# Four graph layers on one core: empty list entries of the GAT layers skipped by their gathers, and their weight factors set to zero in the buffer

## The chip, the cores and the metric

The kernel runs on one core of a Trainium2 chip. The metric is the device time of one execution in microseconds (us); the kernel before took 3435.26 us, the median of three runs (3429.68 to 3435.46).

## What is computed

The input is a batch of 8 graphs' features, x of shape (8, 2048, 128), and one adjacency matrix of 2048 x 2048 that all share, in which an entry is nonzero with probability 1/128. Four layers follow each other. Layers 0 and 1 are graph attention with 8 heads, a feed-forward part and two layer norms. Layers 2 and 3 are the GAT layers, and the change is in them:

```python
h = x @ W
s_i = h @ a_src
s_j = h @ a_dst
e = s_i[:, :, None] + s_j[:, None, :]
e = jnp.where(e >= 0, e, NEG_SLOPE * e)
e = jnp.where(adj[None, :, :] == 0, -jnp.inf, e)
att = jax.nn.softmax(e, axis=-1)
att = jnp.nan_to_num(att, nan=0.0)
out = jnp.einsum('bij,bjd->bid', att, h)
y = out + x
mu = jnp.mean(y, axis=-1, keepdims=True)
var = jnp.mean((y - mu) ** 2, axis=-1, keepdims=True)
return ln_gamma * (y - mu) * jax.lax.rsqrt(var + LN_EPS) + ln_beta
```

A node thus sums the rows h of its neighbours, some 16 on the average, with weights that are a softmax over these neighbours.

## The kernel before, in words

**Lists in place of a matrix.** A first phase (`start`, L862) reads the adjacency matrix, counts each node's neighbours and sorts the 2048 nodes by that count, largest first. The sorted nodes form 16 tiles of 128, one node to a partition. For each tile t, `find_lists` (L349) writes the neighbours of its nodes into `lists`, which has CAPS[t] columns (slots) for that tile: from 30 in tile 0 down to 11 in tile 15, 277 in all. In tile 0 the last two slots are folded: they hold what single nodes have beyond 28. A node with fewer neighbours than slots has empty entries at the end of its list; their index is N = 2048, one past the last node.

**Tables.** For each layer there is a table in the chip's memory with a row per node (`tables`, L306), and the row holds all 8 graphs of the batch. In layers 0 and 1 it has 2048 elements (8,192 bytes). In layers 2 and 3 it has 1040 (4,160 bytes): 8 x 128 of h, and then 16 weight factors, exp(s) and exp(0.2 s) for each graph. The tables of layers 2 and 3 have one row more, number 2048, which `start` fills with zeros (L1031).

**Gathers.** `gather` (L319) is an indirect DMA issued on GpSimd's queue: for each partition it fetches the table row that its entry of one slot names. `bounds_check` is the highest allowed index; an entry above it is not fetched and raises no error. It is N - 1 for layers 0 and 1, so that an empty entry (N) is skipped, and N for layers 2 and 3, so that an empty entry fetches the row of zeros, whose factors of zero give it the weight zero.

**Buffers and chunks.** Slots are worked on in chunks: of up to 2 slots in layers 0 and 1, of up to 4 in layers 2 and 3 (75 chunks a layer). A chunk lies in one of six buffers `kv`, used in turn (`buffer`, L144). `fetch` (L1080) issues the gathers, up to four chunks ahead, as soon as the table rows that a chunk may need are written.

**A GAT chunk** (`gat_chunk`, L728) does this. VectorE multiplies the second factors by the node's own (L745), takes the larger of the two factors as the weight (L746, and once more for the last two graphs, L751), and multiplies h by the weights for graphs 0 to 5 (L757). ScalarE does the same for graphs 6 and 7, one slot and graph at a time (L762). VectorE adds the second half of the slots to the first (L766). TensorE adds the results into an accumulator in PSUM (L772).

**A tile's tail.** After a tile's last chunk come the sums of the weights (L455 to L462), the division (L649) and `gat_tail` (L778): residual and mean on TensorE (L793 to L802), squares on ScalarE (L809), the power -1/2 on GpSimd (L836), the scaling on ScalarE (L817). In layer 2 the rows for layer 3 are made next and written to its table by an indirect DMA on GpSimd's queue (`put_rows`, L494). In layer 3 VectorE multiplies by gamma and adds beta (L850, L852), and an indirect DMA on GpSimd's queue writes the output (L854). There is one buffer `rows` for this, so ScalarE's next squares, which it also takes, wait until the output write before has read it.

**Order.** The order of all instructions on each engine is the order in which the program issues them (`manual_schedule`, L1206; loop in `layers`, L1153). In each step of that loop a chunk's two first parts are issued (with L745 to L751, then L757 and L762), after them the add and the matmuls of the chunk before, and in between one step of every running tail and of `fetch`. GpSimd's queue so holds gathers, table and output writes and the powers of the tails, in order.

Of the kernel before, what the change touches and what calls it, by code (L numbers as in the profile page):

```python
# [8 lines left out]
F32 = mybir.dt.float32  # L9
# [8 lines left out]
P = 128  # L18
B, N, D = 8, 2048, 128
# [9 lines left out]
NB = 8  # L29
CHUNK = 4 * NB * (D + 2)  # L30
KVB = 6
# [51 lines left out]
def sparse_path(ctx: ExitStack, tc: tile.TileContext, ins: dict, out: bass.AP, flag: bass.AP):  # L83
# [10 lines left out]
    nc = tc.nc  # L94
    const = ctx.enter_context(tc.tile_pool(name="const", bufs=1))
    work = ctx.enter_context(tc.tile_pool(name="work", bufs=2))
    small = ctx.enter_context(tc.tile_pool(name="small", bufs=2))
    dram = ctx.enter_context(tc.tile_pool(name="dram", bufs=1, space=bass.MemoryType.DRAM))
# [4 lines left out]
    def misc():  # L103
        return pm.tile([P, 512], F32, tag="m", name="m")
# [9 lines left out]
    nc.vector.tensor_scalar_add(center, ident, -1.0 / P)  # L114
    onesc = const.tile([P, 1], F32, name="onesc")
    nc.vector.memset(onesc, 1.0)
    half = const.tile([P, 8], F32, name="half")
    nc.vector.memset(half, -0.5)

# [21 lines left out]
    bufs = [const.tile([P, CHUNK], F32, name=f"kv{i}") for i in range(KVB)]  # L141
    turn = [-1]

    def buffer():  # L144
        turn[0] += 1
        return bufs[turn[0] % KVB]
# [155 lines left out]
    def width(l):  # L302
        return NB * (2 * D if l < 2 else D + 2)


    tables = [dram.tile([N + (l > 1), width(l)], F32, name=f"table{l}") for l in range(4)]  # L306

    x_rows = ins["x_nodes"]

# [9 lines left out]
    def gather(l, index, dst):  # L319
        nc.gpsimd.indirect_dma_start(  # L320
            out=dst, out_offset=None, in_=tables[l][:, :],
            in_offset=bass.IndirectOffsetOnAxis(ap=index, axis=0),
            bounds_check=N - (l < 2), oob_is_err=False,
        )

    def transpose4(src):
# [115 lines left out]
    def folded_sums(w, box):  # L442

        columns = w.shape[-1]
        ps = misc()[:, :columns]
        for i in range(FOLD):
            nc.tensor.matmul(ps, merge, w[:, i, :], start=i == 0, stop=i == FOLD - 1)
        box["folded"] = small.tile([P, columns], F32, tag="folded", name="folded", bufs=1)
        nc.scalar.copy(box["folded"], ps)
# [275 lines left out]

    def gat_chunk(l, c):  # L728
        box, t, k, ns = c["box"], c["t"], c["k"], c["ns"]
        mine = own[:, t, :]  # L730
        if c["folded"]:
            pf = misc()[:, :NB]
            nc.tensor.matmul(pf, spread, mine, start=True, stop=True)
            mine = small.tile([P, NB], F32, tag="mine", name="mine", bufs=1)
            nc.scalar.copy(mine, pf)
            yield
        if k == 0:
            box["acc"] = pacc.tile([P, NB // 4, 512], F32, tag="acc", name="acc")
            at, n = (0 if t % 2 == 0 else 512 - NB * CAPS[t]), CAPS[t]
            box["w"] = pair[:, at : at + NB * n].rearrange("p (s b) -> p s b", b=NB)  # L740
        acc, w = box["acc"], box["w"]
        hs = c["buf"]
        wc = w[:, k : k + ns, :]
        wa, wb = hs[:, :, NB * D : NB * (D + 1)], hs[:, :, NB * (D + 1) :]
        nc.vector.tensor_mul(wb, wb, mine[:, None, :].to_broadcast([P, ns, NB]))  # L745
        nc.vector.tensor_max(wc, wa, wb)  # L746
        if c["folded"]:
            box["wf"] = small.tile([P, FOLD, NB], F32, tag="wf", name="wf", bufs=1)
            nc.vector.tensor_max(box["wf"], wa, wb)
        ws = small.tile([P, 4, SCALED], F32, tag="ws", name="ws", bufs=3)  # L750
        nc.vector.tensor_max(  # L751
            ws[:, :ns, :], wa[:, :, NB - SCALED :], wb[:, :, NB - SCALED :]
        )
        yield
        hv = hs[:, :, : NB * D].rearrange("p s (b c) -> p s b c", b=NB)
        nv = NB - SCALED
        nc.vector.tensor_mul(  # L757
            hv[:, :, :nv, :], hv[:, :, :nv, :], wc[:, :, :nv, None].to_broadcast([P, ns, nv, D])
        )
        for i in range(ns):  # L760
            for b in range(nv, NB):
                nc.scalar.mul(hv[:, i, b, :], hv[:, i, b, :], ws[:, i, b - nv : b - nv + 1])  # L762
        yield
        left = -(-ns // 2)
        if ns > 1:
            nc.vector.tensor_add(hv[:, : ns - left], hv[:, : ns - left], hv[:, left:ns])  # L766
        yield
        if c["folded"]:
            folded_sums(box["wf"], box)
        for i in range(left):  # L770
            for j in range(NB // 4):
                nc.tensor.matmul(  # L772
                    acc[:, j, :], merge if c["folded"] else ident, hv[:, i, 4 * j : 4 * j + 4, :],
                    start=k + i == 0, stop=c["last"] and i == left - 1,
                )
        yield
# [85 lines left out]
    def start():  # L862
# [165 lines left out]
        )  # L1028
        for i in (3, 4, 5):
            nc.scalar.copy(bufs[i], nil.to_broadcast([P, CHUNK]))  # L1030
        for l in (2, 3):  # L1031
            nc.sync.dma_start(tables[l][N : N + 1, :], bufs[5][:1, : width(l)])


    def verdict():
# [27 lines left out]
    every = []  # L1063
    blocks = [[{} for _ in range(NT)] for _ in range(4)]
    for l in range(4):
        per = 2 if l < 2 else 4
        for t, k, ns, folded in pieces(l, per):
            c = dict(l=l, t=t, k=k, ns=ns, folded=folded, box=blocks[l][t])
            c["last"] = not folded and k + ns == (CAPS[t] if t > 0 else BASE)
            c["run"] = (attention_chunk if l < 2 else gat_chunk)(l, c)  # L1070
            every.append(c)
    now = [0, 0]
# [7 lines left out]
    def fetch():  # L1080

        while now[1] < len(every):
            c = every[now[1]]
            l, t, k, ns = c["l"], c["t"], c["k"], c["ns"]

            if now[1] - now[0] > (4 if now[1] >= KVB and every[now[1] - KVB]["l"] > 1 else 3):
                return
            resorted = l > 0 and t < 2 and not c["folded"]
            need = NT - max([b for end, b in EARLY[t] if k + ns <= end] + [0] if resorted else [0])
            if put[l] < need:  # L1090
                return
            c["buf"] = buffer()[:, : ns * width(l)].rearrange("p (s c) -> p s c", s=ns)
            for i in range(ns):
                at = t * BASE if resorted else first[t]
                index = (sorted_lists if resorted else lists)[:, at + k + i : at + k + i + 1]
                gather(l, index, c["buf"][:, i])
            now[1] += 1
# [6 lines left out]
    def slot():  # L1104
        advance(threads)
        advance(tails)
        fetch()
        beat[0] += 1
        if beat[0] % 3 == 0 and hurry():
            advance(tails)  # L1110
# [42 lines left out]
    def layers():  # L1153
        threads.append(find_lists(0))
        state(0, 0)
        drain()
        fetch()
        begin(every[0])
        drain()
        threads.append(find_lists(1))  # L1160
        for i in range(len(every) + 2):
            now[0] = i
            fetch()
            c2, c1, c, n1, n2 = (chunk(i + j) for j in range(-2, 3))
            if c["k"] == 0:
# [40 lines left out]
    with tc.manual_schedule():  # L1206
        start()
        layers()
# [521 lines left out]
```

## Time and profile before

| | |
|---|---|
| median of three runs | 3435.26 us |
| the profiled execution | 3404.58 us |
| its span, first to last instruction | 3402.8 us |
| VectorE, TensorE, GpSimd, ScalarE busy | 90%, 81%, 65%, 42% of the span |
| mean granted clock of TensorE | 0.918 |
| moved by DMA | 986.52 MB, 290 GB/s |
| read from memory, written | 937.16 MB, 91.55 MB |
| layer 2, from its first product L757 to the first gather of layer 3 that waited for its last writes | about 2,231 to 2,773 us |
| layer 3 | from there to the end |

Profile and trace are of one execution. In them PE is TensorE's matmuls, PEld its weight loads, DVE VectorE, ACT ScalarE, POOL GpSimd; L757 is line 757 of the kernel before. A group of instructions is shown as line, engine, operation, output<-inputs with their shapes, and the count after an x; behind the bar its busy time in us and the mean ns of one, then the idle time of the engine just before these instructions, and what ended most of it. In a timeline the first two columns are start and duration in us. In a list of waits the columns are the total in us, the number of times, and the longest. The buffers `kv0` to `kv5` are all called kv.

### The profile page before, as it was taken

Reading aid. Unit: us, or ns where it says so; the run is one execution under the profiler, and the core shown is the slowest. Engines: PE = TensorE matmul, PEld = TensorE weight load, DVE = VectorE, ACT = ScalarE, POOL = GpSimd, SP = SyncE. Lnnn points to the kernel's source line nnn. Section 1 sums busy time; section 2 is a strip of 40 time slices with the busy share of each in tenths; the row PEclk is TensorE's granted clock in tenths of the full one; section 3 lists DMA queues with packets and bytes.
Section 4 is the critical chain, followed back from the end, with each engine's and each line's share of the span. In section 5 each row is a group of like instructions: output and inputs, shape, how many; then the busy total and the mean of one; then the engine's idle time right before and its main releaser. Section 6 shows DMA issues by size and latency. Waiting matters only on the chain.

```text
span 3402.8 us, 34669 instructions
## 1 busy us (share of the span) xinstructions
PE 2743.1 (81%) x10618; PEld 1582.9 (47%) x10618; DVE 3058.3 (90%) x2695; ACT 1426.6 (42%) x4972; POOL 2207.9 (65%) x1453
## 2 busy tenths in 40 slices
PE   5647888878989997788888989986888976667675
PEld 4523445545555553455545555653445543233332
DVE  7789999999999999999999999976788866889885
ACT  5711333334444442233333444543555654444444
POOL 0065788588657655455676666646787865788773
PEclk9878999999999998899999999998899988888887
DMA  8587787888888777688887888767999986899883
GB/s 336 188 333 266 292 292 282 314 298 288 308 315 299 290 262 295 226 328 295 303 321 295 295 309 299 265 206 250 321 352 346 347 327 223 292 314 330 300 284 112
DMA packets 200625, 986.52 MB, mean 290 GB/s; under 512 B 31918, under 2 KB 33712, under 8 KB 128436
## 3 DMA queue, kind: packets, MB, share of 16 engines
q0 software_dynamic: 175024, 890.45, 72.4%
q1 hardware_dynamic: 20502, 75.52, 5.9%
q10 hardware_dynamic: 4904, 18.24, 1.4%
q8 instruction: 87, 1.43, 0.2%
q14 instruction: 108, 0.88, 0.1%
HBM read 937.16 MB, written 91.55 MB: 302 GB/s over the span
## 4 chain that ended last, share of the span: by engine, by line
DVE 32%; PE 25%; issue 18%; DMA 10%; POOL 5%; ACT 3%; POOLq 0%; DVEq 0%; ACTq 0%
DVE kv L620 11%; DVE kv L606 11%; PE acc L630 8%; PE acc L772 6%; DMA kv<-table,lists 4%; POOL kv L320 3%; DMA kv<-table,sorted_lists 3%; DVE sc L609 2%; PE m L712 2%; DVE kv L766 2%; DMA table<-rows,perm 2%; DVE kv L757 2%; PE m L329 2%; DVE sums L455 1%; DMA out_dram<-rows,perm 1%
## 5 line engine op out<-in xcount | busy, mean ns | idle before, releaser
L320 POOL DMA_INDIRECT kv<-table,lists x955 | 1450.0, 1518 | 357.2 <-issue 206.7
L630 PE MATMUL acc<-kv,ident 128*128 128x512 f32 x2200 | 1107.7, 634 | 222.1 <-DVE kv L620 221.9
L772 PE MATMUL acc<-kv,ident 128*128 128x512 f32 x1184 | 610.1, 667 | 188.6 <-DVE kv L766 155.4
L630 PEld LDWEIGHTS acc<-kv,ident 128*128 128x128 f32 x2200 | 413.7, 202 | 655.1 <-issue 367.5
L606 DVE TENSOR_TENSOR kv<-kv,q 128x2048 f32<-128x2048 f32 (+1 forms) x282 | 629.2, 2231 | 18.7 <-DMA kv<-table,lists 9.7
L609 DVE TENSOR_REDUCE sc<-kv 128x128 f32<-128x2048 f32 (+1 forms) x284 | 634.0, 2232 | 9.2
L620 DVE TENSOR_TENSOR kv<-kv,w 128x2048 f32<-128x2048 f32 (+1 forms) x284 | 631.4, 2223 | 4.9 <-ACT w L615 4.8
L772 PEld LDWEIGHTS acc<-kv,ident 128*128 128x128 f32 x1184 | 243.6, 215 | 504.7 <-issue 285.1
L757 DVE TENSOR_TENSOR kv<-kv,pair 128x3072 f32<-128x3072 f32 (+1 forms) x150 | 466.1, 3108 | 1.0
L476 POOL TENSOR_TENSOR rs<-ss,half 128x4 f32<-128x4 f32 x128 | 221.2, 1728 | 325.4 <-ACT n L471 324.6
L766 DVE TENSOR_TENSOR kv<-kv 128x2048 f32<-128x2048 f32 (+1 forms) x150 | 296.0, 1974 | 129.0 <-ACT kv L762 129.0
L762 ACT ACTIVATE kv<-kv,ws 128x128 f32<-128x128 f32 x1108 | 339.0, 406 | 163.7 <-DVE ws L751 105.5
L471 ACT ACTIVATE n<-m,eps 128x128 f32<-128x128 f32 x512 | 181.0, 366 | 427.1 <-PE m L712 217.4
L615 ACT ACTIVATE w<-sc,lmask 128x64 f32<-128x64 f32 x554 | 165.0, 351 | 455.3 <-DVE sc L609 454.7
L320 POOL DMA_INDIRECT kv<-table,sorted_lists x153 | 204.9, 1339 | 113.0 <-PE acc L630 41.3
L480 ACT ACTIVATE n<-m,rs 128x128 f32<-128x128 f32 x512 | 146.0, 370 | 109.4 <-POOL rs L476 109.0
L494 POOL DMA_INDIRECT table<-rows,perm x57 | 100.2, 1758 | 134.6 <-ACT rows L545 33.5
L329 PE MATMUL m<-ident,n 128*128 128x128 f32 x640 | 106.2, 288 | 73.5 <-ACT n L817 57.2
L712 PE MATMUL m<-w_L_w,hT 128*128 128x128 f32 x1024 | 156.2, 275 | 0.0
L329 PEld LDWEIGHTS m<-ident,n 128*128 128x128 f32 x640 | 82.3, 147 | 140.6 <-ACT n L817 69.0
L712 PEld LDWEIGHTS m<-w_L_w,hT 128*128 128x128 f32 x1024 | 134.9, 192 | 0.0
L691 PE MATMUL m<-n1T,w_L_gnn_W 128*128 128x512 f32 x256 | 131.5, 597 | 0.8 <-ACT n1T L686 0.4
(241 smaller groups left out, 3459.5 us busy)
## 6 DMA issues: line engine op xcount, KB each, us to landing
kept<-xT SPq DMA_DIRECT2D x48, 512.0 KB, 7.4
xT<-kept SPq DMA_DIRECT2D x48, 512.0 KB, 6.8
kv<-in_adj_dram SPq DMA_DIRECT2D x16, 1024.0 KB, 6.7
table<-kv ACTq DMA_DIRECT2D x16, 1024.0 KB, 5.0
kv<-table,lists POOLq DMA_INDIRECT x955, 7.1
kv<-in_x_nodes_dram SPq DMA_DIRECT2D x16, 512.0 KB, 5.8
kv<-table,sorted_lists POOLq DMA_INDIRECT x153, 6.3
found<-cand POOLq DMA_DIRECT2D x16, 64.0 KB, 4.0
```

Of the source, the lines that this page charges most:

```text
L320: nc.gpsimd.indirect_dma_start(out=dst, out_offset=None, in_=tables[l][:, :], in_offset=bass.IndirectOffsetOnAxis(ap=index, axis=0), bound ...
L329: nc.tensor.transpose(pt[:, j * P : (j + 1) * P], src[:, j, :], ident)
L476: nc.gpsimd.tensor_tensor(rs, ss, half[:, :4], op=ALU.pow)
L606: nc.vector.tensor_mul(kk, kk, q[:, None].to_broadcast([P, ns, NB, D]))
L609: nc.vector.tensor_reduce(sc[:, :ns].rearrange("p s (b h) -> p (s b) h", h=NH), kk.rearrange("p s b (h j) -> p (s b) h j", h=NH), axis=AX. ...
L620: nc.vector.tensor_mul(vv, vv, w[:, k : k + ns, :].rearrange("p s (b h) -> p (s b) h", h=NH)[:, :, None, :] .to_broadcast([P, ns * NB, HD, ...
L630: nc.tensor.matmul(acc[:, j, :], merge if c["folded"] else ident, kv[:, i, 4 * j : 4 * j + 4, D:], start=k + i == 0, stop=c["last"] and i ...
L712: nc.tensor.matmul(y[:, j, :], hT[:, f, j, :], wt["2"][:, f, :], start=False, stop=f == 1, skip_group_check=True,)
L757: nc.vector.tensor_mul(hv[:, :, :nv, :], hv[:, :, :nv, :], wc[:, :, :nv, None].to_broadcast([P, ns, nv, D]))
L762: nc.scalar.mul(hv[:, i, b, :], hv[:, i, b, :], ws[:, i, b - nv : b - nv + 1])
L766: nc.vector.tensor_add(hv[:, : ns - left], hv[:, : ns - left], hv[:, left:ns])
L772: nc.tensor.matmul(acc[:, j, :], merge if c["folded"] else ident, hv[:, i, 4 * j : 4 * j + 4, :], start=k + i == 0, stop=c["last"] and i = ...
```

## The change

In layers 2 and 3 an empty entry is no longer fetched. The bounds check of every gather is N - 1, and the row of zeros, with the two small DMAs that wrote it, is gone. In the place of an empty entry the buffer now keeps what it held. So that its weight is zero all the same, the 16 factors of all four slots of a buffer are set to zero after use: `gat_weights` is a view of these 4 x 16 columns, and a copy on ScalarE from a constant zero column, issued after the products L762 of the chunk, clears them for the buffer's next turn. The first six chunks of layer 2 find buffers that layer 1 used; for these a memset on GpSimd, ahead of the chunk's gathers, clears the factors. The h part of an empty entry is whatever was there and is multiplied by zero.

```diff
+    nought = const.tile([P, 1, 1], F32, name="nought")
+    nc.vector.memset(nought, 0.0)
...
-    tables = [dram.tile([N + (l > 1), width(l)], F32, name=f"table{l}") for l in range(4)]
+    tables = [dram.tile([N, width(l)], F32, name=f"table{l}") for l in range(4)]
...
-            bounds_check=N - (l < 2), oob_is_err=False,
+            bounds_check=N - 1, oob_is_err=False,
...
+    def gat_weights(buf):
+
+        return buf[:, : 4 * width(2)].rearrange("p (s c) -> p s c", s=4)[:, :, NB * D :]
+
     def gat_chunk(l, c):
...
         for i in range(ns):
             for b in range(nv, NB):
                 nc.scalar.mul(hv[:, i, b, :], hv[:, i, b, :], ws[:, i, b - nv : b - nv + 1])
+
+        nc.scalar.copy(gat_weights(c["whole"]), nought.to_broadcast([P, 4, 2 * NB]))
         yield
...
-        for l in (2, 3):
-            nc.sync.dma_start(tables[l][N : N + 1, :], bufs[5][:1, : width(l)])
...
-            c["buf"] = buffer()[:, : ns * width(l)].rearrange("p (s c) -> p s c", s=ns)
+            c["whole"] = buffer()
+            c["buf"] = c["whole"][:, : ns * width(l)].rearrange("p (s c) -> p s c", s=ns)
+            if l == 2 and every[now[1] - KVB]["l"] == 1:
+                nc.gpsimd.memset(gat_weights(c["whole"]), 0.0)
```

## The prediction

> **What bounds the kernel now.** I read the page first, then the busy time by window inside the two GAT layers (2,225 us to the end), then the waits of VectorE there, and last the timelines at the places where a wait ends on a DMA. From the page, the whole run and the queue that the change makes lighter:
>
> ```profile
> PE 2743.1 (81%) x10618; PEld 1582.9 (47%) x10618; DVE 3058.3 (90%) x2695; ACT 1426.6 (42%) x4972; POOL 2207.9 (65%) x1453
> q0 software_dynamic: 175024, 890.45, 72.4%
> L757 DVE TENSOR_TENSOR kv<-kv,pair 128x3072 f32<-128x3072 f32 (+1 forms) x150 | 466.1, 3108 | 1.0
> L762 ACT ACTIVATE kv<-kv,ws 128x128 f32<-128x128 f32 x1108 | 339.0, 406 | 163.7 <-DVE ws L751 105.5
> ```
>
> VectorE is the fullest engine. The 150 GAT chunks take 150 L757 products and 1108 ScalarE products L762. Windows of layer 2 (first two) and layer 3 (third); columns are busy us of PE, PEld, DVE, ACT, POOL, then TensorE clock, DMA share, GB/s:
>
> ```profile
> 2500.00:2700.00 200.00, 176.39 (x673) 98.10 (x673) 177.57 (x190) 118.08 (x464) 161.21 (x124) 0.97 0.96 349
> 2700.00:2760.00 60.00, 57.74 (x253) 34.41 (x252) 53.01 (x65) 40.29 (x160) 49.21 (x39) 1.00 0.97 365
> 3050.00:3350.00 300.00, 223.45 (x560) 102.47 (x559) 258.93 (x278) 133.09 (x517) 225.64 (x166) 0.86 0.87 299
> ```
>
> The DMA engines look full (0.96) in layer 2, and that would promise much. But a full resource bounds only if someone waits for it. VectorE's waits from 2,225 us on (total, times, longest):
>
> ```profile
> DVE kv L766 <- ACT kv L762: 129.0, 39, 10.8
> DVE kv L745 <- DMA kv<-table,lists: 40.4, 9, 23.7
> DVE rows L850 <- ACT rows L817: 35.9, 13, 12.2
> DVE o L649 <- PE acc L772: 18.7, 13, 6.2
> DVE kv L745 <- DMA kv<-table,sorted_lists: 17.2, 9, 8.9
> ```
>
> Gathers end only 57.6 us of it, and of that 34.8 are three waits at 2,267, 2,285 and 2,327 us, where layer 2 still waits for its table to be written, and 7.1 is the same at 2,870. About 15.7 us are landings late by 1 to 2.4 us. Most waits are for ScalarE, which stands in order behind two things: the GpSimd power of a tail (161 us of ScalarE's waits), and in layer 3 the landing of the output write (111.5 us). So the GAT layers are held by VectorE, with GpSimd's queue close behind.
>
> **What the Trainium skill says.** DMA: Bandwidth & Descriptors, The descriptor swizzle: a transfer of 128 partitions gives every one of the 16 engines 8 fixed partitions, 0-63 to engines 0-7. No view here shows engines, but it matters: nodes are sorted by degree, so empties sit in high partitions and engines 0-7 are relieved least. ScalarE: Activation LUTs, What ACT_TABLE_LOAD costs: an activation with immediates takes 186 ns + 0.833 ns an element, and back-to-back ones overlap by 93 ns. The trace agrees roughly: the 128x8 copy L547 has a median of 187 ns, the 128x64 Exp with a bias operand 351. GPSIMD Engine Reference, 8. Key points: GpSimd shares its SBUF interfaces with VectorE, with contention under instructions of two SBUF inputs. The trace agrees: of the 134 GAT gathers that took over 1.2 us to issue (median of all 0.997), 104 began while the two-input add L766 ran. Issue time therefore isn't set by the number of rows; gathers of wholly empty and full lists have the same median in layer 3 (0.993 and 1.000).
>
> **Part 1, rows not fetched.** Counted from the inputs, a layer's lists have 277 x 128 = 35,456 entries for 32,733 edges: 2,723 empty (7.7%), 9 slots wholly empty, always a tile's last one. The trace's DMA records have 75,776 packets of 4,160 bytes: 2 x 35,456 gathered and 4,864 written rows, so empties move today. Of 8,192 bytes there are 67,898: 2 x 32,733 gathered and 2,432 written, so layers 0 and 1 do skip theirs by the same bounds check, and the change will work. It removes 5,446 packets, 22.7 MB; at a mean of 0.188 us on 16 engines that is 64 us of DMA time. By the swizzle the least relieved engine loses 101 of 2,216 packets a layer: 2 x 101 x 0.188 = 38 us for both. A wholly empty gather landed 2.1 us after issue in layers 0 and 1 at its quickest, against about 7.0 in layers 2 and 3. Where does this reach the end?
>
> (a) Hand-over of layer 2 to 3. GpSimd's timeline:
>
> ```profile
> 2760.59 0.99 POOL L320 DMA_INDIRECT kv<-table,lists  x1 [0.30 <-issue]
> 2761.88 0.99 POOL L320 DMA_INDIRECT kv<-table,lists  x1 [0.30 <-issue]
> 2763.18 2.48 POOL L494 DMA_INDIRECT table<-rows,perm  x1 [0.31 <-issue]
> 2773.28 1.02 POOL L320 DMA_INDIRECT kv<-table,sorted_lists  x1 [7.62 <-DMA table<-rows,perm]
> ```
>
> The table write lands 9.3 us after issue behind three gathers with 46, 98 and 128 empties; elsewhere 4.3 with quiet queues. On engines 0-7 these drop from 24 packets to about 12: 12 x 0.166 (median packet) = 2.0 us. GpSimd, the power behind it, ScalarE and VectorE (10.8 us idle at 2,785.6) all follow. -2.0 (0 to -2.8).
>
> (b) The end. The same three lists stand ahead of an output write, on which ScalarE and then VectorE wait:
>
> ```profile
> 3341.42 1.01 POOL L854 DMA_INDIRECT out_dram<-rows,perm  x1 [0.30 <-issue]
> 3348.15 0.37 ACT L809 ACTIVATE rows<-m,eps 128x128 f32<-128x128 f32 x1 [12.23 <-DMA out_dram<-rows,perm]
> 3353.39 2.29 DVE L766 TENSOR_TENSOR kv<-kv 128x2048 f32<-128x2048 f32 x1 [4.04 <-ACT kv L762]
> ```
>
> It lands in 6.6 us against 4.4 for the last but one, at 3,379.6: -1.8 (0 to -2.2).
>
> (c) Four late landings at 2,696 to 2,744, 5.8 us together, where tiles 12 to 14 end in wholly empty slots and DMA is at 0.97. TensorE (57.7 of 60 busy) is late next, so I take half: -3.0 (0 to -5.8). (d) The wait of 2.4 at 2,990.5 ends when the wholly empty slot of tile 3 lands; the slot before was issued 1.3 earlier: -1.2 (0 to -2.4). (e) The chunks of tile 0 with 93 to 115 empties a slot, waits 0.97 and 1.16: half, as GpSimd's issue is late next: -1.0. (f) Output writes of layer 3 directly behind a nearly empty gather (at 3,019, 3,085, 3,115); those at 3,189 to 3,310, where VectorE waits longest, have full lists ahead and gain nothing: -2.0 (0 to -4). Sum -11.0.
>
> **Part 2, ScalarE's copy, 128x64, once a chunk.** Not in the trace. Price by the skill 186 + 53 - 93, about 0.15 us in a row; from above 0.35 (the Exp). I take 0.25: 150 x 0.25 = 37.5 us of ScalarE. It follows the products L762, needs nothing that they don't need, and lies beside L757: 8 products take 2.45, the product on VectorE 3.35, so 0.25 fits into 0.9. Behind it on ScalarE stand the tail's squares, copies and the next chunk's products. Without cover, where ScalarE is already late (39 + 13 waits), each costs up to 0.25: 13. Most of these follow an idle stretch of ScalarE in which the copy has long run, so +2.0 (0 to 13). A gather's wait moves from a product to the copy behind it, of a chunk that is over when the buffer comes round: 0.
>
> **Part 3, six memsets on GpSimd** ahead of layer 2's first gathers. Nearest row: memset L870, 128x64, 0.141: 0.85; with the contention above up to 2.3 each: 14. They wait only for VectorE's reads, which the gather behind them waits for as well; queued behind are gathers, table writes and powers. GpSimd is idle for 57 of 100 us there: +0.5 (0 to 14). **The rest**: one memset at the start, two 4 KB writes gone from SP's queue, a table shorter by a row: 0, hidden by the first phase's loads; without that cover under 0.5.
>
> **Sum.** -11.0 + 2.5 = -8.5 against the profiled execution's 3404.58 (span 3402.8 and 1.8 around it): 3396.1. The median of the runs, 3435.26, lies 30.7 higher; I carry the difference over: 3426.8.
>
> **Rivals.** *DMA sets the pace*: the share of 0.96 speaks for it, the few waits on landings against. Whole effect on the least relieved engine 38 us; with two thirds of it, 25: 3410. *Hidden by prefetch*: four chunks are ahead, and each shortened wait is refilled by GpSimd's issue or TensorE; the 129 us for ScalarE speak for it. Gain 1: 3434. *Slower*: the copy stands between the products and the add L766. That decides once it ends after L757, so if it is ordered behind L757 as writing the same buffer, or starts over 0.65 us late: 0.25 and about 0.1 of hand-over in half the chunks, 75 x 0.35 = 26, less 11: 3450. Against it: L762, too, writes between L757's columns, and at 3,111.43 both begin at once.
>
> **Numbers.** Forecast 0.50 (own range 3420 to 3434), DMA pace 0.16, hidden 0.22, slower 0.12. The measurement tells about 0.2% (6.9 us) from no change. Of the forecast 0.6 lies below 3428.4, with DMA's pace: faster 0.46. Its other 0.4 and hidden: same 0.42. Slower 0.12. The range 3410 to 3440 leaves out the slower case and half of DMA's.
>
> **What would show it.** 4,160-byte packets 70,330; q0 at 867.8 MB; the wait at 2,773 down from 7.6 to about 5.6; the four at 2,696 to 2,744 halved; L762's count and L766's 129 us about as before. I am wrong if L766 waits much longer for ScalarE, if the copy takes over 0.4 us, or if the time between layers grows.

## The result, and the profile after

| | before | after |
|---|---|---|
| median, us | 3434.22 | 3427.71 |
| runs, lowest to highest | 19, 3424.04 to 3441.48 | 19, 3417.52 to 3437.23 |
| ratio, 95% interval | | 0.9978, 0.997 to 0.9987 |
| the profiled execution: time, span | 3404.58, 3402.8 | 3428.15, 3426.3 |

The ratio says 7.6 us less (4.5 to 10.3 by its interval); 8.5 were forecast. The two profiled executions differ the other way, and must not be subtracted: judged by TensorE's clock, their chips were not alike. In the series below the kernel before took 3434.87 us on one chip, and 3407.16, 3407.92 and 3405.7 on others. Between the profiled executions it is layer 2 that makes the difference, and there TensorE's granted clock differs. The windows of layer 2, of the kernels before and after, show it (columns as in the prediction: after the lengths PE, PEld, DVE, ACT, POOL, then TensorE clock, DMA share, GB/s):

```profile
2230.30:2788.60 558.30, 453.31 (x1756) 258.42 (x1756) 436.25 (x463) 300.15 (x1163) 406.02 (x318) 0.91 0.87 310
```

```profile
2235.80:2818.50 582.70, 475.82 (x1756) 272.43 (x1756) 436.13 (x462) 311.49 (x1237) 403.67 (x322) 0.88 0.81 278
```

The second is 24.4 us longer with 22.5 us more of PE for the same 1,756 matmuls, and a clock of 0.88 for 0.91. This would hide the change. So the profile after is read against that of a kernel of experiment 3, which has the change's copies but skips nothing and ran at the same clock:

```profile
2232.60:2820.80 588.20, 472.69 (x1756) 271.04 (x1755) 436.26 (x462) 311.29 (x1237) 405.59 (x323) 0.88 0.83 295
```

Against this, layer 2 is 5.5 us shorter in the changed kernel, in one execution of each, at 278 GB/s in place of 295: by these figures some 7% less data and 1% less time.

Lines moved: the products L757 and L762 are now L762 and L767, the add L766 is L773, the squares L809 are L816, and the copy is L769. The page after, on the lines that the prediction began with:

```profile
PE 2765.5 (81%) x10618; PEld 1596.4 (47%) x10618; DVE 3058.6 (89%) x2696; ACT 1448.9 (42%) x5122; POOL 2216.0 (65%) x1459
q0 software_dynamic: 175024, 867.82, 70.6%
L762 DVE TENSOR_TENSOR kv<-kv,pair 128x3072 f32<-128x3072 f32 (+1 forms) x150 | 466.2, 3108 | 1.0
L767 ACT ACTIVATE kv<-kv,ws 128x128 f32<-128x128 f32 x1108 | 341.1, 406 | 170.6 <-DVE ws L756 102.1
```

ScalarE has 150 instructions more (the copies), GpSimd six more (the memsets, 0.14 to 0.17 us each, 0.95 together). The queue q0 moves 867.8 MB, as forecast, and the DMA records hold 70,330 packets of 4,160 bytes, exactly the number forecast. The page's count of packets in q0, 175,024, did not change: in the place of a skipped row stands a packet of 4 bytes. The records hold 36,035 of these, and 30,591 before; that is 5,444 more, for 5,446 empty entries. Their median is 9 ns, that of a row 161 ns. The copy's own line (durations: lowest, median, highest ns):

```profile
L769 ACT COPY kv<-nought x150: 226/240/292, 2253.9 to 3383.6; 128x64 f32<-128x64 f32 x150
```

VectorE's waits from 2,225 us on, after:

```profile
DVE kv L773 <- ACT kv L767: 117.5, 34, 10.2
DVE o L650 <- PE acc L779: 36.6, 14, 6.1
DVE rows L857 <- ACT rows L824: 34.8, 13, 11.2
DVE kv L750 <- DMA kv<-table,lists: 33.3, 9, 21.2
DVE kv L750 <- DMA kv<-table,sorted_lists: 21.9, 6, 8.9
```

The add's wait hardly changed: 117.5 us for ScalarE and 14.0 us more for which the list names no releaser, 131.5 together, against 129.0 before. The wait for TensorE's sums (36.6 us for 18.7) goes with the slower clock: the kernel of experiment 3 has 35.8. The two waits on gathers make 55.2 us together, against 57.6: with 7.7% of the rows gone, VectorE waits for rows nearly as long as before. The gain shows most at two places. The first is the hand-over from layer 2 to 3, where the table write of tile 12 stands behind the last gathers of tile 15. GpSimd's timeline:

```profile
2793.28 0.99 POOL L321 DMA_INDIRECT kv<-table,lists  x1 [0.30 <-PE acc L779]
2794.58 0.99 POOL L321 DMA_INDIRECT kv<-table,lists  x1 [0.30 <-issue]
2795.88 1.00 POOL L495 DMA_INDIRECT table<-rows,perm  x1 [0.30 <-issue]
2801.93 1.03 POOL L321 DMA_INDIRECT kv<-table,sorted_lists  x1 [5.04 <-PE acc L779]
```

From the start of the table write (L495) to the next gather it was 10.10 us; it is 6.05. Part of that is the write's own issue, 1.00 for 2.48, which is no effect of the change: the kernel of experiment 3 issues it in 1.00, too, and still takes 9.70. The releaser named here, PE, had long been done; what ended the wait is the landing of the write, whose last packet ended 4.85 us after its issue. The second place is near the end, at the output write of tile 12, which is the fourth last and the last with gathers ahead of it:

```profile
3368.70 1.01 POOL L861 DMA_INDIRECT out_dram<-rows,perm  x1 [0.30 <-issue]
3372.17 0.37 ACT L816 ACTIVATE rows<-m,eps 128x128 f32<-128x128 f32 x1 [8.84 <-DMA out_dram<-rows,perm]
3377.42 2.29 DVE L773 TENSOR_TENSOR kv<-kv 128x2048 f32<-128x2048 f32 x1 [0.81 <-ACT kv L767]
```

From the issue of the output write to ScalarE's squares it was 6.72 us (3,341.42 to 3,348.15 in the prediction's lines); it is 3.47, and VectorE's wait behind it falls from 4.04 to 0.81.

### The profile page after: what moved, and what is told of

Read it like the earlier page. It is cut to its first block, busy times and chain, and to the rows that moved or that the text cites. A ratio compares the mean times of both kernels' runs of the same rounds, so it can differ in the third digit from the quotient of the medians.

```text
span 3426.3 us, 34787 instructions
## 1 busy us (share of the span) xinstructions
PE 2765.5 (81%) x10618; PEld 1596.4 (47%) x10618; DVE 3058.6 (89%) x2696; ACT 1448.9 (42%) x5122; POOL 2216.0 (65%) x1459
## 3 DMA queue, kind: packets, MB, share of 16 engines
q0 software_dynamic: 175024, 867.82, 70.6%
## 4 chain that ended last, share of the span: by engine, by line
DVE 36%; PE 23%; issue 19%; DMA 8%; POOL 5%; ACT 3%; POOLq 0%; DVEq 0%; ACTq 0%
DVE kv L621 13%; DVE kv L607 12%; PE acc L779 8%; PE acc L631 5%; POOL kv L321 3%; DMA kv<-table,lists 3%; DVE sc L610 2%; DVE kv L773 2%; DMA kv<-table,sorted_lists 2%; DVE kv L762 2%; PE m L713 1%; DVE sums L456 1%; PE m L330 1%; PE m L528 1%; DMA out_dram<-rows,perm 1%
## 5 line engine op out<-in xcount | busy, mean ns | idle before, releaser
L762 DVE TENSOR_TENSOR kv<-kv,pair 128x3072 f32<-128x3072 f32 (+1 forms) x150 | 466.2, 3108 | 1.0
L477 POOL TENSOR_TENSOR rs<-ss,half 128x4 f32<-128x4 f32 x128 | 234.9, 1835 | 315.2 <-ACT n L472 314.3
L773 DVE TENSOR_TENSOR kv<-kv 128x2048 f32<-128x2048 f32 (+1 forms) x150 | 296.2, 1975 | 131.6 <-ACT kv L767 117.5
L767 ACT ACTIVATE kv<-kv,ws 128x128 f32<-128x128 f32 x1108 | 341.1, 406 | 170.6 <-DVE ws L756 102.1
L495 POOL DMA_INDIRECT table<-rows,perm x57 | 94.4, 1656 | 130.5 <-ACT rows L546 32.9
```

What stands on the lines that cost most here:

```text
L477: nc.gpsimd.tensor_tensor(rs, ss, half[:, :4], op=ALU.pow)
L762: nc.vector.tensor_mul(hv[:, :, :nv, :], hv[:, :, :nv, :], wc[:, :, :nv, None].to_broadcast([P, ns, nv, D]))
```

## The experiments

Theory, after the result: the gain comes from writes that stood in the DMA queue behind nearly empty gathers, and most of it from tile 15; the copies cost next to nothing. Rivals: a lighter DMA gains everywhere (rows in proportion); the copy's cost eats a larger gain; or the single row of zeros, fetched by 5,446 entries, was itself slow. In the table every ratio is to the kernel before on the same chip.

| | kernel | before, us | us | ratio, 95% interval |
|---|---|---|---|---|
| 1 | only tile 15's empties skipped | 3434.87 | 3427.86 | 0.9979, 0.9971 to 0.9987 |
| 2 | all but tile 15's skipped | 3434.87 | 3429.73 | 0.999, 0.9982 to 0.9999 |
| 3 | copies, nothing skipped | 3434.87 | 3435.72 | 1.0, 0.9991 to 1.0009 |
| 4 | all skipped, no copies | 3434.87 | 3425.32 | 0.9979, 0.9966 to 0.9992 |
| 5 | nearly no row fetched | 3407.16 | 3375.76 | 0.9901, 0.9885 to 0.9917 |
| 6 | before, with 128 rows of zeros | 3407.16 | 3412.08 | 1.0017, 1.0008 to 1.0026 |
| 7 | after, two halves of the output buffer | 3407.16 | 3367.67 | 0.9882, 0.9864 to 0.9899 |
| 8 | before, two halves | 3407.16 | 3367.68 | 0.9881, 0.9864 to 0.9897 |
| 9 | tile 15 of layer 2 only | 3407.92 | 3405.89 | 0.9993, 0.9984 to 1.0002 |
| 10 | tile 15 of layer 3 only | 3407.92 | 3402.58 | 0.9984, 0.9977 to 0.9992 |
| 11 | after, every copy eight times | 3407.92 | 3393.64 | 0.9966, 0.9953 to 0.9979 |
| 12 | two halves, every copy eight times | 3405.7 | 3369.49 | 0.9894, 0.9877 to 0.991 |

**1. Tile 15 alone.** All of the change is kept, and the row of zeros too; the bounds check skips the empties of the last tile only, 610 of the 5,446 rows.

```diff
-            bounds_check=N - 1, oob_is_err=False,
+            bounds_check=N - skip, oob_is_err=False,
...
-                gather(l, index, c["buf"][:, i])
+                gather(l, index, c["buf"][:, i], l < 2 or t == NT - 1)
```

> The changed kernel, with its copies and memsets, but the row of zeros is kept and only the empties of tile 15 are skipped in layers 2 and 3 (610 of 5,446 rows, 11%). Theory (the gain is at the two ends of a layer, where a write stands behind tile 15's nearly empty gathers): 5 to 7 us below the kernel before, table write at the hand-over followed by the next gather after about 6 us, VectorE's wait at the last output write under 1 us. Rival (DMA engines set the pace, every row saved counts alike): 11% of the gain less the copies, so within 2 us of the kernel before.

Measured: 7.2 us less than before (4.5 to 10.0), as much as the whole change with 11% of its rows. Its timelines, GpSimd and ScalarE:

```profile
2789.14 1.00 POOL L495 DMA_INDIRECT table<-rows,perm  x1 [0.30 <-issue]
2795.39 1.02 POOL L321 DMA_INDIRECT kv<-table,sorted_lists  x1 [5.25 <-DMA table<-rows,perm]
...
3372.31 0.37 ACT L816 ACTIVATE rows<-m,eps 128x128 f32<-128x128 f32 x1 [8.84 <-DMA out_dram<-rows,perm]
```

Both waits are as short as in the full change. It follows that rows do not count in proportion: 11% of them would then have given 0.8 us.

**2. All but tile 15.** The same with `t < NT - 1` in place of `t == NT - 1`: 4,836 rows skipped.

> The changed kernel with the row of zeros kept for tile 15 alone: the other 4,836 empties (89%) are skipped. Theory of the two ends: within 3 us of the kernel before, the table write at the hand-over again followed by 10 us of GpSimd's waiting. Rival of DMA pace: 89% of the gain, 5 to 7 us faster.

Measured: 3.4 us less (0.3 to 6.2), for 89% of the rows, so these rows are worth something, too. The wait at the end stays (6.35 us from the output write to the squares), that at the hand-over is between (8.30). The gains of 1 and 2 add up to 10.6 where both at once gave 7.6; the intervals (about 3 us either way on each) are wide enough for that.

**3. Copies alone.** The same with `l < 2`: the copies and memsets stay, every empty entry fetches its zeros.

> The kernel before with the copies on ScalarE and the memsets on GpSimd added, and nothing skipped. Prediction's step: 2.5 us slower than the kernel before. Rival (the copy stands in VectorE's way): 15 to 25 us slower, VectorE's waits for ScalarE's products up by as much from 129 us.

Measured: no difference (within 3.1 us either way). Its timelines at the two places:

```profile
2795.86 1.00 POOL L495 DMA_INDIRECT table<-rows,perm  x1 [0.30 <-issue]
2805.56 1.02 POOL L321 DMA_INDIRECT kv<-table,sorted_lists  x1 [8.70 <-DMA table<-rows,perm]
...
3378.13 0.37 ACT L816 ACTIVATE rows<-m,eps 128x128 f32<-128x128 f32 x1 [11.88 <-DMA out_dram<-rows,perm]
```

Both waits are long again, so they belong to the rows and not to the copies.

**4. No copies.** The change without its copy on ScalarE.

```diff
-        nc.scalar.copy(gat_weights(c["whole"]), nought.to_broadcast([P, 4, 2 * NB]))
```

> The changed kernel without the 150 copies on ScalarE, so that an empty entry counts with the factors that an earlier chunk left in its slot (the GAT sums are then not the reference's). Prediction's step: about 2 us faster than the changed kernel, so 8 to 10 below the kernel before. Rival that the copies cost nothing: equal to the changed kernel, 6 to 7 below. Rival that they cost much: 15 or more below.

Measured: 0.9979 beside 0.9978 with the copies. 3 and 4 agree from both sides that 150 copies of 0.24 us, 36 us of ScalarE, cost nothing that shows (3 us either way in 3, 5 in 4). So a much larger gain that the copies ate is excluded; one of 2 us isn't.

**5. Nearly no row fetched.** The limit of the rival that DMA sets the pace.

```diff
-            bounds_check=N - 1, oob_is_err=False,
+            bounds_check=N - 1 if l < 2 else 0, oob_is_err=False,
...
```

> The changed kernel with a bounds check of 0 in layers 2 and 3, so that their gathers are issued as before but fetch only node 0's row; the factors are set to 0.5 in place of 0 and the flag for the other path is forced off (the results of layers 2 and 3 are left out of the computation: they are made of what lay in the buffers). It shows all that DMA traffic of gathers can be worth in these layers. Theory that landings matter only where a write stands behind gathers or a first gather is waited for: 20 to 50 us below the changed kernel for 92% of the rows, not more, since VectorE, GpSimd's issue and TensorE stay. Rival of DMA pace (7 us for the 8% of the change, in proportion): 80 us or more.

Measured: 33.7 us less than before, about 26 less than the changed kernel (0.9901 / 0.9978), for the whole of the remaining gathers. Its page and VectorE's waits:

```profile
q0 software_dynamic: 175024, 595.93, 48.7%
```

```profile
DVE kv L773 <- ACT kv L767: 123.6, 41, 10.1
DVE kv L750 <- DMA kv<-table,lists: 24.0, 4, 19.8
DVE kv L750 <- DMA kv<-table,sorted_lists: 8.5, 6, 2.1
```

272 MB fewer than after, and the add still waits 123.6 us for ScalarE. If DMA set the pace, 80 us or more were expected. Since all remaining rows together are worth 26 us, 7.7% spread evenly would be worth some 2 (an estimate in proportion): that the change gained 7.6 is a matter of place. Even of the 26 us the larger part is in layer 3. From the start of its first chunk to that of its last this kernel takes 545.5 us and the changed one 562.2, and ScalarE's wait for the output write is 62.5 us in place of 98.0:

```profile
ACT rows L816 <- DMA out_dram<-rows,perm: 62.5, 8, 10.7
```

**6. A row of zeros for each partition,** on the kernel before. Every empty entry fetches row N + p of 128 rows of zeros in place of the one row N.

```diff
+        each = small.tile([P, 48], F32, tag="each", name="each")
+        nc.vector.tensor_scalar(
+            each[:, :s], top[:, :s], 0.0, node[:, 0:1], op0=ALU.is_equal, op1=ALU.mult
+        )
+        nc.vector.tensor_add(far[:, :s], far[:, :s], each[:, :s])
...
```

> The kernel before, nothing skipped, but 128 rows of zeros in place of one: the empty entry of partition p fetches row 2048 + p, so that no two of a gather read the same row. Tells apart why the writes behind tile 15 landed 3.2 to 4 us earlier where 12 packets of 0.166 us on the fullest engine give 2.0. If it is the number of packets alone: same as the kernel before, 6.5 us from the last output write to ScalarE's squares, 9.7 to 10.1 at the hand-over. If reading one row from many packets at once is slow: each about 1 us shorter, no packets of 0.9 us or more behind tile 15's last gathers, and up to 3 us less in all.

Measured: 5.8 us more. The two new groups of instructions cost 7.0 us of VectorE, which is enough to account for it:

```profile
L394 DVE TENSOR_SCALAR each<-top,node 128x18 f32<-128x18 f32 (+12 forms) x16 | 4.2, 263 | 0.0
L397 DVE TENSOR_TENSOR far<-far,each 128x18 f32<-128x18 f32 (+12 forms) x16 | 2.8, 178 | 0.6
```

And the waits stay. At the hand-over, on GpSimd's timeline:

```profile
2773.92 2.48 POOL L499 DMA_INDIRECT table<-rows,perm  x1 [0.30 <-issue]
2783.20 1.02 POOL L320 DMA_INDIRECT kv<-table,sorted_lists  x1 [6.80 <-DVE ws L756]
```

It is 9.28 us from write to gather, and 5.93 from the output write of tile 12 to the squares. These are the shortest of the kernels that fetch all empties (9.66 to 10.10, and 6.51 to 6.79), so a part of up to 0.8 us may be due to the one row; but the skipped rows took off 3. Single packets of 1.1 to 1.8 us remain, too. That one row is read by all is not the main cause of the waits.

**7 and 8. Two halves of the output buffer,** after and before. ScalarE's waits for an output write come from the one buffer `rows`; here even and odd tiles of layer 3 take halves of another buffer, which is idle then.

```diff
-            n = rows_of(box)[:, : B * D].rearrange("p (b d) -> p b d", d=D)
+            n = rows_of(blocks[3][0])[:, t % 2 * B * D : (t % 2 + 1) * B * D]
+            n = n.rearrange("p (b d) -> p b d", d=D)
```

> The changed kernel with layer 3's output rows in two halves of one buffer by turns, so that ScalarE's squares wait for the output write of two tiles before and not of the last. Theory (VectorE waits in layer 3 mostly because ScalarE stands behind the output write): ScalarE's 98 us of waiting for it gone, 20 to 35 us faster than the changed kernel. Rival (the next wait, GpSimd's power or VectorE itself, is right behind): under 7 us faster.

> The same two halves in the kernel before. Theory: 20 to 35 us faster than the kernel before; the change's gain beside it falls by the 3 us of the end, so that the changed kernel with two halves is some 4 us below this one. Rival that the gain is spread over all tiles: 7 us below as without the halves.

Measured: 40 us less in both, 3367.67 and 3367.68, where 20 to 35 were expected. From ScalarE's waits with the change and halves the output write is gone:

```profile
ACT kv L767 <- DVE ws L756: 105.7, 28, 10.2
ACT n L825 <- POOL rs L844: 97.5, 15, 11.0
ACT rows L825 <- POOL rs L844: 80.1, 13, 12.4
```

From the start of layer 3's first chunk to that of its last it is 528.9 and 529.9 us, and was 568.2. Of the change's gain nothing is seen beside the halves, but with these intervals less than some 8 us can't be told, so that this says little on the hand-over. At the end nothing is left to gain, since no one waits for the write: ScalarE takes the next squares without it (their second half begins 1.42 and 1.53 us after its issue).

**9 and 10. The two places apart.** As 1, in layer 2 only (`t == NT - 1 and l == 2`), and in layer 3 only.

> As the kernel that skips tile 15's empties alone, but in layer 2 only (305 rows): the write to layer 3's table is relieved, the last output writes are not. If the 3.7 us that the hand-over's wait lost reach the end: 3 to 4 us below the kernel before, GpSimd's gap at the hand-over 6.2 us, the last output write to ScalarE's squares still 6.5. Rival (layer 3 takes it back, as its first chunks wait for the next table write anyway): 0 to 1 us below.

> The same for layer 3 only (305 rows). If the 3.2 us at the last output write reach the end: 3 us below the kernel before, gap at the hand-over 10 us, output write to squares 3.5. Rival (TensorE's last sums are late anyway): 0 to 1 us below.

Measured: 2.4 us less (5.5 less to 0.7 more), and 5.4 less (2.7 to 7.8). The traces show each wait shortened in its own kernel and long in the other: 6.73 and 9.69 us at the hand-over, 6.78 and 3.46 at the end. The end is shown to reach the time, and the traces agree: the output write after this one follows 18.06 to 18.08 us later in the four kernels with one output buffer and one copy or none that skip these rows, and 20.5 to 21.4 us later in the five that fetch them. The hand-over is shortened, but whether that reaches the time this pair doesn't settle. The traces say that it reaches VectorE: from the hand-over's write to the start of layer 3's fifth chunk it is 64.3 to 65.1 us in five kernels that skip the rows and 65.7 to 68.0 in six that fetch them. Further on the ranges overlap.

**11. Eight copies.** To see how much cover the copy has.

```diff
-        nc.scalar.copy(gat_weights(c["whole"]), nought.to_broadcast([P, 4, 2 * NB]))
+        for _ in range(8):
+            nc.scalar.copy(gat_weights(c["whole"]), nought.to_broadcast([P, 4, 2 * NB]))
```

> The changed kernel with the copy on ScalarE eight times a chunk in place of once. Seven more of about 0.15 us in a row are 1.05 us, so products and copies take 3.6 us beside VectorE's 3.35. Prediction's step (a copy is free while it fits into the 0.9 us that VectorE's product leaves): little for the first five or six, then late, in all 15 to 45 us above the changed kernel. Rival (ScalarE has room everywhere, since it idles half the time): under 5 us. Rival (every copy is on the path): 158 us.

Measured: 0.9966, not slower at all, so the 15 to 45 us more that were expected are excluded. Beside the changed kernel's 0.9978 it is 4 us less, with 5 us either way by the two intervals, so that a gain is not shown. ScalarE's timeline at two chunks of layer 3:

```profile
3199.64 2.18 ACT L770 COPY kv<-nought 128x64 f32<-128x64 f32 x8
3201.72 2.17 ACT L825 ACTIVATE rows<-m,rs 128x128 f32<-128x128 f32 x8
3203.73 2.47 ACT L767 ACTIVATE kv<-kv,ws 128x128 f32<-128x128 f32 x8
3206.07 2.19 ACT L770 COPY kv<-nought 128x64 f32<-128x64 f32 x8
```

Eight take 2.18 us, 0.27 each. The next products start behind them, and VectorE's add doesn't wait longer for it: 116.9 us in all, with 131.5 in the changed kernel, whose trace is of a slower chip.

```profile
DVE kv L774 <- ACT kv L767: 116.9, 43, 10.1
```

What has become less is ScalarE's wait for the output write. The changed kernel, then this one, whose trace is of the quickest of its eight executions:

```profile
ACT rows L816 <- DMA out_dram<-rows,perm: 98.0, 11, 15.1
```

```profile
ACT rows L817 <- DMA out_dram<-rows,perm: 59.0, 9, 11.4
```

**12. Halves and eight copies.** If there is a gain in 11 and it runs through the output write, it must go when no one waits for that.

> The two halves of the output rows and the eight copies together, on the changed kernel. Eight copies alone came out 0.12% of the whole below the changed kernel where 15 to 45 us above were expected, with ScalarE's waits for the output write down from 98 to 59 us. If that is where the gain came from (a later ScalarE meets the output write when it has landed), it is gone here, since with two halves nothing waits for that write: then 5 to 40 us slower than two halves with one copy (0.988 of the kernel before), by what the copies stand in VectorE's way. Rival (the copies help in another way, by evening out TensorE's or the DMA engines' load): again some 10 us faster than the two halves alone, 0.985 or less.

Measured: 0.9894, beside 0.9882 with halves alone (halves and copies 4 us more, 8 either way). A further gain to 0.985 is excluded; so is the larger part of the 5 to 40 us expected. 1,050 more copies of 0.27 us, 284 us of ScalarE, cost between nothing and some 12 us even with the output write out of the way.

## Why the prediction was right, point by point

The sign, the size (8.5 forecast, 7.6 measured, 3 us either way) and the main mechanism were right: writes with a reader stood behind nearly empty gathers. That the sum came so near is in part luck, for single steps missed on both sides: (b) was too small by 1.2 us, (c) too large by 1.3, and the 2.0 us charged for the copies did not show. The waits below are read at the same instruction in the traces of all kernels with one copy or none, experiment 5 left out, as means: those in which the row's empties are fetched (five to seven), and those that skip them (four or five). For (b) they are those with one output buffer.

| step | forecast | kept | skipped | change |
|---|---|---|---|---|
| (a) table write to next gather | -2.0 | 9.46 | 6.42 | -3.0 |
| (a) VectorE's wait behind it | | 9.85 | 7.36 | -2.5 |
| (b) output write to squares; VectorE's wait | -1.8 | 6.5; 3.8 | 3.5; 0.8 | -3.0; -3.0 |
| (c) late rows of tiles 12 to 14, layer 2 | -3.0 | 6.4 | 4.7 | -1.7 |
| (d) slot of tile 3 and the next chunk | -1.2 | 2.5 | 1.2 | -1.3 |
| (e) four chunks of tile 0, both layers | -1.0 | 36.3 | 35.5 | -0.8 |

**(a) and (b), the writes behind empty lists: right, (a) at about its size, (b) too small.** In (a) the traces mix two lengths of the write's own issue, 1.00 and 2.48 us. Among those with the same length VectorE's wait fell by 1.8 and 2.3 us, which is the forecast, and the gap to the next gather by 2.8 and 3.0. (b) was taken from the last but one output write as the floor, 4.4 us. No gathered row stood ahead of that one, but one of its own packets took 1.13 us; in traces where none is that long it takes 3.5. The floor measured for (b) is 3.46 to 3.47, in four kernels.

The packets' records of (b) show the wait itself. Before the change 209 gathered rows still had to start when the write was issued. The last of them ended 5.01 us after that, and the write's last packet 1.25 us later, at 6.26. In the other four kernels that fetch these rows the last row ended at 4.25 to 5.08, and the write again 1.25 later in each. After the change 9 rows were left, and the last ended at 0.56; the write's packets began at 1.58, after all rows, and ended at 3.01. The count "12 x 0.166 = 2.0", made for (a), fell short here: the last row ended about 4 us earlier, not 2, of which the write could use 3. Why it is twice the count stays open. Single long packets don't explain it: before the change 11 of these rows took over 0.4 us, eight of them 0.9 to 1.3, but in experiment 3 four did, none over 0.85, and its write ended at 6.03. The descriptor swizzle of the Trainium skill's DMA: Bandwidth & Descriptors, by which (a) was counted, is seen here as far as start times can tell, for the records name no engine: the last slot that fetches anything has 30 rows, on the first partitions, and these went as about four packets each on 7 to 8 engines, one after the other, with the other engines idle.

**(c) too large, (d) right.** Of the late rows a quarter went, not half. TensorE or GpSimd's issue is not what holds the rest: in experiment 5, which issues the same gathers but fetches next to nothing, these waits are gone. They are for the rows of full entries, which the change leaves.

**(e) wrong in its place.** The wait of 1.16 us in layer 3 belonged to a chunk whose slots have few empties. What did fall was the wait of the folded chunk ahead of these, 23.66 to 21.18 and 7.12 to 4.12, and the next chunk's rose by nearly as much, 1.04 to 3.04 and 1.11 to 4.57. A wait was moved, not removed. **(f) not resolved:** ScalarE's waits for output writes are 97.0 to 101.1 us with all skipped or all but tile 15 and 104 to 120 otherwise in kernels with one buffer and one copy or none, which allows for a good part of the -2.0 to -4, but those of tile 15 are in it.

**The copy: the price right, the cover wrong.** 0.240 us, 0.25 was taken; ScalarE: Activation LUTs, What ACT_TABLE_LOAD costs gives 186 + 53 = 239 ns without the overlap. In a row there is no overlap to be seen, 0.27 each. The cover was said to be 0.9 us beside VectorE's product, and +2.0 to come from where it lacks. Experiments 3 and 4 put the cost at 0, 3 to 5 either way, and 11 shows that 2.2 us per chunk fit. The reason lies in the order of the program: behind a copy stand the next chunk's products and at times a tail's squares or scalings, and the products must be done by the next chunk's add. So the cover is VectorE's whole period of a chunk, about 6 us at the least (3.35 for the product, 2.28 for the add, 0.54 for the weights), less 2.45 for the products, and not the product alone.

**The rivals.** *DMA sets the pace* falls by 5 (26 us for 92% of the rows left) and by 1 against 2. *Hidden by prefetch* is right for most of the other 89% of the rows, which gave 3.4 us in experiment 2, and wrong for tile 15's, behind whose lists there is no prefetch but a write with a reader. *Slower* falls by 3, 4 and 11: the copy does not come between the products and the add. That the change doesn't do what it says falls by the 70,330 packets. (Before it, the records hold 75,778, two more than the prediction's sum, which left out the two writes of the row of zeros.)

**What stays open:** how much of the hand-over's 2 to 3 us reaches the end (2.4, 3 either way); why the last rows behind tile 15 take twice the count, and why single packets are long; and whether eight copies gain anything, and by what steps they shorten ScalarE's wait for the output write.

## What to carry to other kernels

That a resource is 0.96 busy doesn't say what relieving it is worth: ask who waits for it, and look for the few places where something with a reader waiting stands behind the load. Here 11% of the rows, ahead of two writes, gave 7.2 us, and all of them 7.6. The larger lever was another wait, which the prediction had listed: the one output buffer of layer 3, cut into two halves, takes 1.2% off with or without the change (0.9882 and 0.9881), five times as much. When a wait is shortened, look at the next one on the same engine before it is counted: in tile 0 it took back nearly all.

## What the runs showed that was not expected

Work added to ScalarE did not slow the kernel: eight copies a chunk raise its busy time by two thirds in the middle of layer 3. The window of the kernel with eight copies, then of the changed one:

```profile
3000.00:3100.00 100.00, 70.12 (x179) 31.89 (x178) 90.26 (x88) 75.66 (x304) 82.60 (x62) 0.86 0.89 309
```

```profile
3000.00:3100.00 100.00, 69.98 (x183) 31.85 (x182) 87.44 (x90) 45.94 (x184) 83.18 (x60) 0.87 0.90 309
```

ACT goes from 45.94 to 75.66 us, and the other engines' busy times stay within 3 us. And chips differ by more than the change: the kernel before took 3405.7 to 3434.87 us, 0.9%. In the traces TensorE is at half its clock for 92 to 104 us of layer 2 on the quicker chips and for 132 to 145 on the slower one; why they differ is not known.
